# Reading the places of eight fetched batches into SP's registers a superblock ahead of the fetches

## The chip, the cores and the metric

The kernel runs on one core of one Trainium2 chip. The metric is the device time of that core in microseconds (us). Three runs of the kernel before gave 2747.27, 2744.07 and 2747.38 us; their median is 2747.27. All times inside the kernel come from one profiled execution and count from the start of its span.

## The reference

The input x holds 64 batches of 64 tokens with 256 features, and each batch has a type (0, 1 or 2). Two blocks are added to x, one after the other:

```python
x = x + attn(cond(x, itok))          # gated FFN chosen by type + shared one, gated; then attention
x = x + ffn(cond2(x, itok))          # two relu FFNs chosen by type + three shared ones, gated; then top-2 MoE
# in cond:
expert_out = einsum('bsf,bfd->bsd', gelu(h @ wi0[type]) * (h @ wi1[type]), wo[type])
weights = softmax(relu(concat([expert_out[:, 0], share_out[:, 0]]) @ g0) @ g1)
return expert_out * w0 + share_out * w1
```

All of it is in float32. What matters here is that the weights of `cond` and `cond2` depend on the batch's type, and that the result for a batch mixes a typed part and shared parts under a gate that is computed from the batch's first token.

## The kernel before

The kernel sorts the batches by type at the start, so that eight batches, a superblock of 512 tokens, share the weights of one type as far as possible. Eight superblocks (s = 0 to 7) pass through stages: the shared FFN of the first block (names with c), the typed FFN of the first block (names with e, `typed1`), the shared FFNs of the second block (names with d, `shared2`), its typed FFN (names with t, `typed2`), then the router and the MoE. Large products are made with seven half-size products instead of eight (`strassen`; tiles p1 to p7, and sa and sb for the accumulators). Small pieces of other work, above all the gates and the attention of a superblock, are put between the products: `begin_cond(s)` appends the steps of `combine1(s)` and `attention(s)` to a list, and `tick` takes one step from it.

Batches that don't fit their superblock's type are computed apart and laid beside the others in DRAM. So the typed results of a superblock go out to DRAM (`keep_typed`, into spillt) and come back one batch at a time (`fetch_typed`), each from a place that is known only at run time: the integer tile src_i holds it. In the same way the shared results of block one lie in DRAM (spill) in the order of the input and are fetched by `fetch1` in the sorted order, from the places in batch_i. Each of these fetches is a DMA of 64 KB from SP's queue, and in front of each stands a `value_load`, which takes one place from on-chip memory into a register of SP: one load (TENSOR_LOAD), one register operation and one check of the bounds (L1138, L1308). There are 64 fetches from spill and 128 from spillt, in bursts of eight: fetch1(s) once per superblock, fetch_typed(0, s) in the typed FFN of block one, and fetch_typed(1, s) in that of block two.

`fetch_typed` follows `keep_typed` in the `after` step at the end of a superblock (L1155, L1206). `fetch1(0)` is called by `begin_attention`, later ones at the end of the step `sums` of `combine1`, when its sums have read the tile part1. The first reader of what fetch1 and fetch_typed bring is the gate's first step, `hidden`: its matmuls write the tile pha in block one (tiles tw1 and part1) and phb in block two (tw and the third shared part).

SP's queue works in order. Besides these fetches it sends the weights: `send1` and `send2` (calls in `first` and `second` of each item) send the next half weights of 896 KB with their Strassen sums into a ring of five or four slots, and a load waits until TensorE has read what the slot held before. `sum_half` (L903) prepares such weights: it loads two pieces of raw weights, has POOL add four sums (`sum_weights`, L188 to L191) and writes the result to DRAM from POOL's queue (L915). Where a read and its DMA stand in SP's order is fixed by `behind_last`, which puts them behind the last DMA that `sync_dma` recorded. For the other engines a scheduler lays down the order when the program is built, from its own estimates of durations; an engine then takes its instructions in that order. POOL's queue carries, among the rest, a part of the attention: `values` (L1360) multiplies V by two masks (L1370, L1374) and copies halves across partitions by DMA (L1373), and the matmuls that write the tile ov wait for all of these. L1532 are scattered writes of x to the output.

Of the kernel before, what the change touches and what calls it, by code (L numbers as in the profile page):

```python
# [17 lines left out]
NB, S, D, F = 64, 64, 256, 1024  # L18
DC, FC = D // P, F // P
NTYPE = 3  # L20
GB = 4
NSB = NB // (2 * GB)
NG = 2 * GB
NFIX = NTYPE - 1
# [62 lines left out]
def adaln_attn_ffn(ctx: ExitStack, tc: tile.TileContext, a: dict, out: bass.AP):  # L87
    nc = tc.nc
# [9 lines left out]
    def area(kb, *shape):  # L98

        at, n = int(kb * 256), 1  # L100
        for m in shape:
            n *= m
        dims = "abcd"[: len(shape)]
        return arena[:, at : at + n].rearrange(
            f"p ({' '.join(dims)}) -> p {' '.join(dims)}", **dict(zip(dims, shape))
        )
# [21 lines left out]
    def behind_last():  # L128

        return tc.issue_after(paced["last"].ins) if paced else nullcontext()  # L130
# [166 lines left out]
    def of_half(o, g):  # L297

        return lambda op, k, i: o[op][:, k, (2 * g + i) * P : (2 * g + i + 1) * P]
# [121 lines left out]
    K = SimpleNamespace(bias={}, rows_i={})  # L421
# [11 lines left out]
    for j in range(2):  # L433
        t = area(AT_S + 14 * j, DC, F)
# [407 lines left out]
    def prepare_x(s):  # L842
        if s == 1:
            turn_x(1)
        cut_x(s)
# [9 lines left out]
    def keep1(s):  # L855
        part = area(AT_KEEP1 + 4 * (s % 2), DC, NG, S)
        v = spill[0][s * NG : (s + 1) * NG].rearrange("b p (c t) -> c p b t", c=DC)
        for c in range(DC):
            sync_dma(v[c], part[:, c])
# [10 lines left out]
    for s in range(NSB):  # L870
        its = layer(
            f"c{s}", 2, lambda g: [of_half(o, g) for o in up1],
            lambda g: lambda op, k: down1[op][:, 2 * g + k, :], lambda s=s: xblocks[s],
            AT_HOPS1, area(AT_KEEP1 + 4 * (s % 2), DC, SB), lambda s=s: keep1(s),
            (lambda s=s: prepare_x(s + 1)) if s + 1 < NSB else lambda: cut_e(0), ticks="odd",
        )
# [60 lines left out]
    def send_half(st, k, j, q, w, at):  # L937

        if (st, k) not in xes:
            with behind_last():  # L940
                r = nc.sync.value_load(K.utype_i[0:1, NSB + k : NSB + k + 1], min_val=0, max_val=NTYPE - 1)
                at_k = nc.sync.value_load(K.fix_i[0:1, k : k + 1], min_val=0, max_val=(NB - 1) * S)
            xe = area((AT_XE if st else AT_XEF) + 2 * (k % 2), DC, BT)
            n = P if k else BT
            sync_dma(xe[:, :, 0:n], X[:, :, bass.ds(at_k, n)])
            xes[st, k] = (xe, r)
        r = xes[st, k][1]
        rows = slice(q * F // 2, (q + 1) * F // 2)
        if w[0] == "i":
            t = area(at, DC, F // 2)  # L950
            src = a["L0_cond2_expert_wi"] if st else a[f"L0_cond_Wi{w[1]}"]
            src = src[bass.ds(r + j if st else r, 1), :, rows].rearrange("e (c p) f -> p (e c) f", p=P)
        else:
            t = area(at, FC // 2, D)
            src = a["L0_cond2_expert_wo"] if st else a["L0_cond_Wo"]
            src = src[bass.ds(r + j if st else r, 1), rows, :].rearrange("e (c p) d -> p (e c) d", p=P)
        sync_dma(t, src)
        ring[st, k, j, q, w] = t
# [31 lines left out]
    def send1():  # L990
        if sent1[0] == len(queue1):
            return
        kind, n, *w = queue1[sent1[0]]
        at = AT_RING1 + 7 * (sent1[0] % NRING1)
        sent1[0] += 1
        if kind == "f":
            send_half(0, n, 0, *w, at)
        elif kind == "s":
            send_share0(w[0], n, at)
        else:  # L1000
            s, g = divmod(n, 2)
            if s not in types1:
                with behind_last():
                    types1[s] = nc.sync.value_load(K.utype_i[0:1, s : s + 1], min_val=0, max_val=NTYPE - 1)
            sync_dma(
                area(at, 7 * 256), sums1[w[0]][g][bass.ds(types1[s], 1)].rearrange("e p n -> p (e n)")
            )
            ring1[n, w[0]] = half_blocks(w[0][0], at)
# [120 lines left out]
    def keep_typed(st, at, n):  # L1129
        v = spillt[st][at : at + n].rearrange("b p (c t) -> c p b t", c=DC)  # L1130
        for c in range(DC):
            sync_dma(v[c], (tp if st else tp1)[:, c, 0 : n * S].rearrange("p (b t) -> p b t", t=S))

    def fetch_typed(st, s):
        for b in range(NG):
            n = s * NG + b
            with behind_last():
                r = nc.sync.value_load(K.src_i[0:1, n : n + 1], min_val=0, max_val=NB + NFIX * GB - 1)  # L1138
                sync_dma(
                    (tw if st else tw1)[:, :, b * S : (b + 1) * S],  # L1140
                    spillt[st][bass.ds(r, 1)].rearrange("e p (c t) -> p (e c) t", c=DC),
                )

    def cut_e(s):
        xblocks["e", s], _ = column_blocks(X, s * SB, area(AT_XSUME, 4, HB))
# [3 lines left out]
    def typed1(s, ahead):  # L1149


        def ups(g):
            return [lambda op, k, i, w=w: ring1[2 * s + g, w][op][:, k, i * P : (i + 1) * P] for w in ("i0", "i1")]

        def after():  # L1155
            keep_typed(0, s * NG, NG)
            while s and s - 1 not in summed:
                tick()
            fetch_typed(0, s)

        its = layer(
            f"e{s}", 2, ups, lambda g: lambda op, k: ring1[2 * s + g, "o"][op][:, k, :],
            lambda: xblocks["e", s], AT_HOPSE, tp1, after, ahead, AT_STE, None, AT_G1E, "fine",
        )
        for it in its:
            def first(f=it.first):
                r = f()
                send1()
                send1()
                return r  # L1170

            def second(r, f=it.second):
                f(r)
                send1()

            it.first, it.second = first, second
        return its
# [8 lines left out]
    def send2():  # L1186

        if sent2[0] == len(queue2):
            return
        n, w = queue2[sent2[0]]  # L1190
        at = AT_RING2 + 7 * (sent2[0] % NRING2)
        sent2[0] += 1
        s, j, g = n // 4, n // 2 % 2, n % 2
        if s not in utypes:
            with behind_last():
                utypes[s] = nc.sync.value_load(K.utype_i[0:1, s : s + 1], min_val=0, max_val=NTYPE - 1)
        sync_dma(
            area(at, 7 * 256), sums[w][g][bass.ds(utypes[s] + j, 1)].rearrange("e p n -> p (e n)")
        )
        ring2[n, w] = half_blocks(w, at)  # L1200

    def typed2(s, ahead):
        def ups(g):
            return [lambda op, k, i: ring2[4 * s + g, "i"][op][:, k, i * P : (i + 1) * P]]

        def after():  # L1206
            while between:
                tick()
            keep_typed(1, s * NG, NG)
            fetch_typed(1, s)  # L1210

        its = layer(
            f"t{s}", 4, ups, lambda g: lambda op, k: ring2[4 * s + g, "o"][op][:, k, :],
            lambda: xblocks["d", s], AT_HOPS2[2], tp, after, ahead, AT_ST2,
            lambda g: K.wab[g // 2][:, s : s + 1],
        )
        for it in its:
            def first(f=it.first):
                r = f()
                send2()  # L1220
                return r

            def second(r, f=it.second):
                f(r)
                send2()

            it.first, it.second = first, second
        return its
# [3 lines left out]
    for j in range(4):  # L1232
        r = slice(32 * j, 32 * j + 32)
# [69 lines left out]

    def fetch1(s):
        for b in range(NG):
            n = s * NG + b
            with behind_last():
                r = nc.sync.value_load(K.batch_i[0:1, n : n + 1], min_val=0, max_val=NB - 1)  # L1308
                sync_dma(
                    part1[:, :, b * S : (b + 1) * S],  # L1310
                    spill[0][bass.ds(r, 1)].rearrange("e p (c t) -> p (e c) t", c=DC),
                )
# [311 lines left out]
    def begin_attention():  # L1624
        nc.sync.dma_start(out=g0, in_=a["L0_cond_g0"].rearrange("(c p) d -> p c d", p=P))
        nc.sync.dma_start(out=g1, in_=a["L0_cond_g1"].rearrange("(c p) j -> p c j", p=P))
        fetch1(0)

    nc.gpsimd.memset(X[:, :, NB * S : NCOL], 0.0)
# [9 lines left out]
    with tc.issue_after(K.iota.ins):  # L1639
        r = sum_columns(nc.gpsimd, up1[0], slice(0, F // 4))  # L1640
# [20 lines left out]
    for s in range(NSB):  # L1661
        its = typed1(s, (lambda s=s: cut_e(s + 1)) if s + 1 < NSB else lambda: cut_x1(0, 0))
        if s == 0:
            its = typed(0) + its
# [22 lines left out]
    for s in range(NSB):  # L1687
        its = shared2(s, 1)
# [15 lines left out]
    for s in range(NSB):  # L1704
        its = shared2(s, 2) + typed2(s, None if s == NSB - 1 else lambda s=s: cut_x1(s + 1, 2))
# [84 lines left out]
    for n, _ in enumerate(router(0)):  # L1790
        if n >= 17 and behind:
            f, _ = behind.pop(0)
# [300 lines left out]
```

## Time and profile before

| what | us |
|---|---|
| median of three runs | 2747.27 |
| the profiled execution, by the same clock | 2744.14 |
| its span in the profile | 2742.5 |
| TensorE busy (PE) | 2709.1 |
| VectorE busy (DVE) | 1626.9 |
| GpSimd busy (POOL) | 1065.2 |
| ScalarE busy (ACT) | 837.1 |
| mean granted TensorE clock | 0.999 |

A line of a view gives the source line, the engine and the operation, the tiles as written<-read, and the count. "PEld" is TensorE's weight load, "SPq" is an instruction in SP's queue, most often one that issues a DMA. In the timeline the first two columns are the start and the duration of a run of equal instructions, and the bracket at the end of a line is the idle time of the engine before it and what ended that time. Nearly all tiles are parts of one large on-chip buffer and appear as "arena". All matrix products are recorded under L119, the one line that issues them, so the tile's name tells them apart.

The five stretches that matter: the first block's shared FFN lasts until about 314 us, its typed FFN with the attention until about 840, then come the shared FFNs of block two (the first beside the last of the attention), the typed FFN of block two until about 1940, and the router and the MoE.

### The profile page before, as it was taken

The page shows a single profiled execution, that of the slowest core. Times are in us where ns is not written, and L with a number is a line of the kernel's source. Part 1 is how long each engine was busy: PE and PEld are TensorE (multiplying, and loading weights), DVE is VectorE, ACT ScalarE, POOL GpSimd, SP SyncE. Part 2 cuts the span into 40 slices and gives each one's busy share as a digit, 9 for nine tenths or more (in the row PEclk, how much of TensorE's full clock was granted, in tenths as well). Part 3 has the DMA queues.
Part 4 walks back from the last instruction along what each step waited for, and adds up shares of the span by engine and source line. Part 5 has one row for each costly group of instructions (what it writes and reads, how often), then busy time and mean ns, then how long its engine had stood idle before and what let it go on. Part 6 is the DMA issues. An engine that isn't in the chain of part 4 may idle for free.

```text
span 2742.5 us, 38338 instructions
## 1 busy us (share of the span) xinstructions
PE 2709.1 (99%) x13765; PEld 2232.6 (81%) x13765; DVE 1626.9 (59%) x2931; ACT 837.1 (31%) x1535; POOL 1065.2 (39%) x1121
## 2 busy tenths in 40 slices
PE   8999999999999999999999999999999999999998
PEld 7888887677767778888888888888888888877777
DVE  7887467888887774535546766667443333332443
ACT  2221124544444332212222222222222222322333
POOL 4555123343335667634323332325323322324332
PEclk9999999999999999999999999999999999999999
DMA  4554545343342123652443434444200000013330
GB/s 118 159 173 141 191 149 185 97 128 128 104 147 88 63 101 135 207 183 81 154 136 126 150 132 146 147 139 135 70 17 6 9 5 6 5 52 79 96 92 2
DMA packets 236365, 293.47 MB, mean 107 GB/s; under 512 B 141624, under 2 KB 199824, under 8 KB 236048
## 3 DMA queue, kind: packets, MB, share of 16 engines
q1 hardware_dynamic: 214608, 231.44, 26.9%
q0 software_dynamic: 21344, 58.54, 6.3%
q8 instruction: 109, 1.79, 0.3%
q10 hardware_dynamic: 224, 1.05, 0.1%
q14 instruction: 80, 0.66, 0.1%
HBM read 208.80 MB, written 83.99 MB: 107 GB/s over the span
## 4 chain that ended last, share of the span: by engine, by line
PE 91%; DVE 4%; issue 2%; DMA 2%; ACT 0%; SPq 0%; POOL 0%; POOLq 0%; DVEq 0%; ACTq 0%
PE sad L119 6%; PE p5r L119 5%; PE p1r L119 5%; PE po L119 5%; PE sbd L119 4%; PE sat L119 4%; PE p5d L119 3%; PE p1d L119 3%; PE sbt L119 3%; PE p6r L119 2%; PE p4r L119 2%; PE p7r L119 2%; PE p5e L119 2%; PE p1e L119 2%; PE p5t L119 2%; PE sac L119 2%
## 5 line engine op out<-in xcount | busy, mean ns | idle before, releaser
L198 POOL TENSOR_TENSOR arena<-arena 128x512 f32<-128x512 f32 (+1 forms) x175 | 236.3, 1350 | 667.2 <-DVE arena L195 659.3
L199 POOL TENSOR_TENSOR arena<-arena 128x512 f32<-128x512 f32 (+1 forms) x175 | 213.5, 1220 | 18.0 <-DVE arena L196 17.0
L119 PE MATMUL sad<-arena 128*128 128x256 f32 x768 | 176.7, 380 | 0.0
L119 PE MATMUL po<-arena 128*128 128x256 f32 (+1 forms) x704 | 169.8, 399 | 0.1
L119 PEld LDWEIGHTS sad<-arena 128*128 128x128 f32 x768 | 144.0, 190 | 19.6 <-issue 0.8
L119 PEld LDWEIGHTS po<-arena 128*128 128x128 f32 x704 | 132.9, 190 | 28.4 <-issue 11.0
L119 PE MATMUL p5r<-arena 128*128 128x256 f32 x640 | 149.7, 381 | 0.5 <-DVE arena L256 0.5
L119 PE MATMUL p1r<-arena 128*128 128x256 f32 x640 | 150.0, 382 | 0.0
L195 POOL TENSOR_TENSOR arena<-arena 128x256 f32<-128x256 f32 (+1 forms) x55 | 45.1, 821 | 260.8 <-ACT arena L1740 80.7
L1902 POOL DMA_INDIRECT xs<-arena,slot_i x64 | 62.6, 978 | 199.9 <-ACT arena L1898 108.7
L119 PEld LDWEIGHTS p1r<-arena 128*128 128x128 f32 x640 | 120.0, 190 | 21.2 <-issue 5.9
L119 PEld LDWEIGHTS p5r<-arena 128*128 128x128 f32 x640 | 120.8, 190 | 17.6 <-DVE arena L256 1.4
L119 PE MATMUL sbd<-arena 128*128 128x256 f32 x576 | 134.8, 381 | 0.0
L195 DVE TENSOR_TENSOR arena<-arena 128x512 f32<-128x512 f32 (+2 forms) x127 | 96.8, 762 | 63.2 <-ACT arena L332 34.2
L119 PEld LDWEIGHTS sbd<-arena 128*128 128x128 f32 x576 | 108.5, 190 | 17.5 <-POOL arena L199 2.2
L188 POOL TENSOR_TENSOR arena<-arena 128x256 f32<-128x256 f32 (+1 forms) x53 | 47.9, 905 | 184.8 <-DMA arena<-in_L_cond_share_wo 43.3
L119 PE MATMUL sat<-arena 128*128 128x256 f32 x512 | 118.6, 382 | 0.8 <-POOL arena L198 0.8
L196 DVE TENSOR_TENSOR arena<-arena 128x512 f32<-128x512 f32 (+2 forms) x127 | 108.8, 856 | 3.5
L2028 POOL DMA_INDIRECT out<-arena,rows_i x40 | 61.9, 1547 | 123.4 <-ACT arena L2027 66.9
L119 PEld LDWEIGHTS sat<-arena 128*128 128x128 f32 x512 | 96.2, 190 | 14.0 <-POOL arena L198 1.2
L332 ACT ACTIVATE arena<-arena 128x512 f32<-128x512 f32 x144 | 90.3, 628 | 45.6 <-DVE arena L267 21.6
L119 PE MATMUL p5d<-arena 128*128 128x256 f32 x384 | 99.7, 382 | 2.4 <-DVE arena L256 2.4
(452 smaller groups left out, 6243.5 us busy)
## 6 DMA issues: line engine op xcount, KB each, us to landing
arena<-sums_i SPq DMA_DIRECT2D x32, 896.0 KB
arena<-sums_2i SPq DMA_DIRECT2D x32, 896.0 KB
arena<-sums_2o SPq DMA_DIRECT2D x32, 896.0 KB
arena<-in_L_ffn_eW SPq DMA_DIRECT2D x16, 1024.0 KB
arena<-sums_o SPq DMA_DIRECT2D x16, 896.0 KB
spill<-arena SPq DMA_DIRECT2D x24, 512.0 KB
arena<-spill POOLq DMA_DIRECT2D x24, 512.0 KB, 6.1
sums_i<-arena POOLq DMA_DIRECT2D x12, 896.0 KB, 3.9
```

The costliest lines, as they stand in the source:

```text
L119: nc.tensor.matmul(o, lhsT=lhsT, rhs=rhs, start=start, stop=stop, skip_group_check=shared_bank)
L188: eng.tensor_add(s1, a21, a22)
L195: eng.tensor_sub(t1, b12, b11)
L196: r = eng.tensor_sub(t2, b22, t1)
L198: eng2.tensor_sub(t3, b22, b12)
L199: return r.ins, eng2.tensor_sub(t4, b21, t2).ins
L332: nc.scalar.activation(c_out(ij), src, AF.Relu)
L1902: nc.gpsimd.indirect_dma_start(out=to.rearrange("e n w -> (e n) w"), out_offset=bass.IndirectOffsetOnAxis(ap=slot_i[:, n, i : i + 1], axis=0),
L2028: nc.gpsimd.indirect_dma_start(out=out_rows, out_offset=bass.IndirectOffsetOnAxis(ap=row_i[:, u : u + 1], axis=0), in_=eo, in_offset=None, ...
```

## The change

The reads leave the fetch functions. A new function `read_ahead` reads places and keeps the registers in a dictionary; the fetches take them from there. For the typed fetches of superblock s, the reads follow the two `send1` calls of each item's `first` (two and two, so eight over the two items), or the `send2` of each of the four items' `first` in block two (two each). For the fetches of fetch1(s + 1), four reads follow the `send1` in each item's `second` of superblock s. The eight reads for fetch1(0) are made at once in `begin_attention`, directly ahead of the fetches. All reads are still made by SP with the same three instructions, and their number stays 192.

```diff
+    places = {}
+
+    def read_ahead(kind, s, bs):
+        t, top = (K.batch_i, NB) if kind == "part" else (K.src_i, NB + NFIX * GB)
+        for b in bs if s < NSB else ():
+            n = s * NG + b
+            with behind_last():
+                places[kind, n] = nc.sync.value_load(t[0:1, n : n + 1], min_val=0, max_val=top - 1)
+
     def fetch_typed(st, s):
         for b in range(NG):
-            n = s * NG + b
+            r = places.pop((st, s * NG + b))
             with behind_last():
-                r = nc.sync.value_load(K.src_i[0:1, n : n + 1], min_val=0, max_val=NB + NFIX * GB - 1)
                 sync_dma(
...
-            def first(f=it.first):
+            n = its.index(it)
+
+            def first(f=it.first, n=n):
                 r = f()
                 send1()
+                read_ahead(0, s, range(4 * n, 4 * n + 2))
                 send1()
+                read_ahead(0, s, range(4 * n + 2, 4 * n + 4))
                 return r
 
-            def second(r, f=it.second):
+            def second(r, f=it.second, n=n):
                 f(r)
                 send1()
+                read_ahead("part", s + 1, range(4 * n, 4 * n + 4))
...
-        for it in its:
-            def first(f=it.first):
+        for n, it in enumerate(its):
+            def first(f=it.first, n=n):
                 r = f()
                 send2()
+                read_ahead(1, s, range(2 * n, 2 * n + 2))
                 return r
...
     def fetch1(s):
         for b in range(NG):
-            n = s * NG + b
+            r = places.pop(("part", s * NG + b))
             with behind_last():
-                r = nc.sync.value_load(K.batch_i[0:1, n : n + 1], min_val=0, max_val=NB - 1)
                 sync_dma(
...
+        read_ahead("part", 0, range(NG))
         fetch1(0)
```

In the built program the number of instructions of each kind on SP and POOL stays as it was (one wait more on SP), and SP's DMAs keep their order. The other engines' orders differ in two places: one matmul of the tile sae stands behind the first pha instead of ahead of it, and on POOL, in the first stretch of the shared FFN, the sums L188 to L191 of one weight half and its store L915 stand ahead of, instead of behind, a group of L1370, L1374 and L1373 of the last attention superblock.

## The prediction

> **What bounds the kernel now.** First the page's row of busy times: is one engine full?
>
> ```profile
> PE 2709.1 (99%) x13765; PEld 2232.6 (81%) x13765; DVE 1626.9 (59%) x2931; ACT 837.1 (31%) x1535; POOL 1065.2 (39%) x1121
> ```
>
> TensorE is busy for 2709.1 of the 2742.5 us span, so 33.4 us is all that any change can win by removing idle time of TensorE, and a part of that lies ahead of the first matmul and behind the last. Next the waits of TensorE alone, longest first (total us, times, longest):
>
> ```profile
> PE px L831 <- POOL arena L480: 3.9, 1, 3.9
> PE p5d L119 <- DVE arena L256: 2.4, 3, 1.3
> PE pha L119 <- DMA arena<-spillt: 2.3, 1, 2.3
> ```
>
> Only the third line has to do with the transfers that the change touches: one single wait, of 2.3 us, of the gate's matmuls (pha) for the eight fetches out of spillt. The other fifteen rounds of such fetches (seven more for expert layer 1, eight for layer 2, where the gate's tile is phb) stop TensorE nowhere. Then the timeline around that wait, TensorE and SP's DMA issues:
>
> ```profile
> 414.87 0.67 PE L119 MATMUL pha<-arena 128*32 128x256 f32 x8 [2.33 <-DMA arena<-spillt]
> 415.47 2.83 PE L119 MATMUL sae<-arena 128*128 128x256 f32 x6
> 418.09 2.36 PE L119 MATMUL sbe<-arena 128*128 128x256 f32 x8
> 420.28 0.51 PE L119 MATMUL pfa<-fold,arena 128*128 128x8 f32 x4
> ```
>
> ```profile
> 402.38 10.30 SPq L126 DMA_DIRECT2D arena<-spillt  x8
> 413.51 0.99 SPq L126 DMA_DIRECT2D arena<-sums_i  x2
> ```
>
> SP needs 10.30 us to send eight fetches of 64 KB; the last leaves at about 412.1 and pha starts 2.75 us later. And behind the wait the matmuls are slow: 14 of them (6 sae, 8 sbe) take from 415.47 to 420.28, 4.81 us, where the run of 8 sae just before it (410.66) took 1.89 us, some 0.216 each from start to start. The granted clock says why (the last three columns are clock, DMA share, GB/s):
>
> ```profile
> 416.00:418.00 2.00, 2.00 (x6) 1.64 (x5) 0.00 (x0) 0.00 (x0) 1.09 (x1) 0.50 1.03 423
> ```
>
> **The reads that are moved.** A place is read by three SP instructions (durations min/median/max in ns):
>
> ```profile
> L1138 SPq TENSOR_LOAD <-src_i x128: 262/273/1072, 399.5 to 1956.7; - x128
> L1138 SPq FUSED_REGOPS  x128: 152/152/159, 400.4 to 1957.0; - x128
> L1138 SPq SEQ_ASSERT  x128: 18/18/18, 400.6 to 1957.2; - x128
> ```
>
> Together 443 ns. The pitch of the fetches is (10.30 - 0.57)/7 = 1.39 us; their own three instructions (0.037, 0.029 and the DMA's 0.568) take 0.634. What is left, 0.31 us, is hand-over between six instructions, half of it the read's: a read costs 0.60 us, a fetch without it 0.79. Nothing is removed: 192 reads (64 of batch_i, 128 of src_i) x 0.60 = 115 us of SP stay, but leave the bursts.
>
> **Step 1, the first burst.** Its start at 402.38 is set by the landing of the store into spillt, not by the first read. With a pitch of 0.79 the eighth fetch leaves at 402.38 + 7 x 0.79 = 407.9, and with the same 2.75 us pha could start at 410.7. TensorE gets to it at about 412.2 (the built program puts it one sae matmul earlier), so the wait is gone with 1.5 us to spare: 2.3 us. What is next late there? The waits written into the program behind pha are for POOL results that ended at 397.1 and 398.3 and for DVE results that ended at 411.6, all early enough.
>
> Whether the slow clock goes too is worth as much. The Trainium skill ("TensorE: Matmul & The Clock Gate", in the section "Why this matters for your kernels") asks for no idle gap over about 3 us to keep the full clock, and Part 1 has the array throttled after an idle window of about 3.4 us. By that rule a gap of 2.33 us costs no clock and the step is worth 2.3 us. The row shows 0.50 right behind this gap, and the 14 matmuls took 4.81 - 14 x 0.216 = 1.8 us too long. The row decides: step 1 is worth 2.3 + 1.8 = **4.1 us**.
>
> **Step 2, the other fifteen bursts: nothing.** Each ends 4 to 5 us earlier, ahead of gate matmuls that already found their data: pha of the second round starts at 480.8, and its last fetch left at 466.4. If this cover were gone, each would cost up to its lateness; none is near.
>
> **Step 3, where the reads go: nothing.** They stand behind weight loads (send1, send2), two or four at a time, so the load behind them leaves 1.2 or 2.4 us later; a load also waits for its ring slot, and reads in front of such a wait are free. In the timeline the shortest time from a weight load's issue to its first matmul is 6.5 us (352.4 to 358.9, and there SP stood waiting for the slot for 8 us, longer than the two reads), the next 7.7 and 8.1. The load of 7.7 (468.8 to 476.5) follows a burst that ends 4 us earlier and has six reads (3.6 us) put ahead of it, so it keeps its time. The first read of src_i gets a wait for DVE (the sort), which ended long before. Behind a waiting send1, reads only queue with what already queued there. Both ends: up to 1 us either way.
>
> **Step 4, what the reordering does to POOL: about 0.6 us lost.** Engines' instruction orders in the built program are the same except in one place of POOL, and SP's DMAs keep their order. In the first stretch of the shared FFN, POOL makes the masked values of the last attention superblock (L1370, L1374 and the copies L1373), for which TensorE's ov waits, and there the four weight sums L188 to L191 of the next weight half now stand ahead of them instead of behind:
>
> ```profile
> 861.57 1.09 POOL L1532 DMA_INDIRECT out<-arena,row_i  x1 [0.16 <-issue]
> 862.69 0.74 POOL L1370 TENSOR_TENSOR arena<-arena,vrest 128x256 f32<-128x256 f32 x1
> ...
> 873.95 0.99 POOL L188 TENSOR_TENSOR arena<-arena 128x256 f32<-128x256 f32 x1 [6.66 <-DMA arena<-in_L_cond_expert_wi]
> ```
>
> ```profile
> 848.95 10.35 SPq L126 DMA_DIRECT2D arena<-spill  x8
> 860.08 10.02 SPq L126 DMA_DIRECT2D arena<-spillt  x8
> 870.20 1.05 SPq L126 DMA_DIRECT2D arena<-in_L_cond_expert_wi  x2
> ```
>
> ```profile
> 874.23 0.66 PE L119 MATMUL ov<-arena 128*32 128x64 f32 x32
> ...
> 878.78 1.13 PE L119 MATMUL p5d<-arena 128*128 128x256 f32 x4 [0.65 <-DVE arena L256]
> ```
>
> L188 waits for a load that SP sends behind sixteen fetches. Without reads these take 16 x 0.79 = 12.6 us: the load leaves at 848.95 + 12.6 = 861.6 and L188 starts 3.75 us behind it, as before: 865.3. From there to ov, by durations of these rows: L188 1.07, L1532 1.25, L189 to L191 2.2, L1370 0.7, the store L915 0.6, L1532 1.1, first copy 0.55, L1374 0.7, second copy's landing 2.0 (the median of its six here): 10.2 us, so 875.5. TensorE stands before ov at 874.23: 1.3 us of new wait. The wait of 0.65 at 878.78 is for DVE, whose work there does not depend on ov, so it is absorbed: net 0.6. Bounds: 0, if loads come 1.3 us sooner; 2.5 idle with a slow clock behind it, some 3.7 net, if they come 1.2 us later. I take 0.6, since the gap of 1.29 us at 896.2 had clock 1.00 behind it.
>
> **Sum.** -4.1 + 0.6 = -3.5 us. The profiled execution took 2744.14 (span 2742.5 and 1.6 around it), so 2740.6; it is 3.1 below the median of the runs, 2747.27. Carried to the median: **2743.8**.
>
> **Rivals.**
> Rival 1, the stall is dearer in most executions. Two of three runs took 2747.3, 3.2 more than the profile. If that is this stall with more slow clock behind it (the clock is granted by stretches of 3.4 us, so one more costs 1.7), the change takes it away too: 2747.27 - 3.5 - 3.2 = 2740.6. For it: nothing else in the middle of the profile shows a slow clock. Against: the start shows matmuls of 0.43 us up to 12.8 us, which can vary as well.
> Rival 2, the gain is eaten. By the skill's rule the clock is not part of it (2.3), and step 4 costs 2.5 idle with its clock: between -2.3 + 0.6 and -4.1 + 3.7, so 2745.6 to 2746.9, no change that can be told.
> Rival 3, slower: the fetches do not speed up, because a 64 KB transfer and not SP's read sets the pitch; the skill ("DMA: Bandwidth & Descriptors", the section "Issuing engines are not separate DMA queues") calls issue time usually small beside the transfer. Then L188 keeps its start at 873.95, with the whole chain behind it: ov at 884.15, 9.9 us of idle TensorE plus 1.7 of slow clock, less 0.65; step 1 gives nothing, so 2747.27 + 11 = 2758; if only the late burst is stuck, 2754. It decides from a load that leaves SP later than some 869. Against it: the DMA share in a burst is 0.20, and a fetch lands 2.75 us after issue, so three or four would be in flight.
>
> **How the numbers follow.** My case 0.46, rival 1 0.30, rival 2 0.15, rival 3 0.09. Faster or slower counts from 0.2% on (5.5 us), about what a measurement of this kernel can tell from no change. Rival 1 and a fringe of my case (a dearer stall in part, 0.06) are faster; rival 3 is slower; the rest is no change. The likeliest case's own range is 2741.9 to 2746. The range of 8 in 10, 2739.5 to 2748, takes in rivals 1 and 2.
>
> **What would show it.** Right: no wait of pha for spillt, clock 1.00 from 412 to 420, bursts of 6 us, L188 near 865 less the 4 us won. Wrong: bursts still of 10 us (rival 3); a wait of ov for POOL over 2 us with clock 0.50 behind it (rival 2); a profile of after as far below 2740.6 as the run differences (rival 1).

## The result, and the profile after

The kernel became slower by 0.17%: over 20 runs each the median went from 2746.97 to 2750.33 us, and the ratio on record is 1.0017 with a 95% interval of 1.0011 to 1.0023. (The quotient of the two medians is 1.0012. The ratios in this document are the ones on record, with their intervals in brackets; the quotients of the medians lie up to 0.0006 nearer to 1.) The forecast was 2743.8 us, with 2748 as its upper end. The profiled execution of the kernel after took 2751.57 us (span 2749.9, mean clock 0.997).

TensorE is as full as before, by the page's row of busy times; its busy time grew by 2.2 us with the same number of matmuls, so some of them took longer:

```profile
PE 2711.3 (99%) x13765; PEld 2236.9 (81%) x13765; DVE 1625.2 (59%) x2931; ACT 836.9 (30%) x1535; POOL 1069.2 (39%) x1121
```

The first part of the forecast is there. In TensorE's timeline of the kernel after, pha follows the matmul ahead of it with no bracket, and the eight sae behind it take 2.00 us:

```profile
415.04 0.67 PE L119 MATMUL pha<-arena 128*32 128x256 f32 x8
415.63 2.00 PE L119 MATMUL sae<-arena 128*128 128x256 f32 x8
```

SP's timeline shows why: the bursts of eight fetches shrank from 10.3 us to about 6, and so the weight load behind two of them left at 860.60 instead of 870.20:

```profile
405.38 6.26 SPq L126 DMA_DIRECT2D arena<-spillt  x8
...
848.22 5.86 SPq L126 DMA_DIRECT2D arena<-spill  x8
854.26 6.24 SPq L126 DMA_DIRECT2D arena<-spillt  x8
860.60 1.05 SPq L126 DMA_DIRECT2D arena<-in_L_cond_expert_wi  x2
```

But in TensorE's waits the 2.3 us of pha have given way to a longer one:

```profile
PE p5d L119 <- ACT arena L1381: 5.0, 1, 5.0
```

The kernel after has 14 lines more at this place, so L1381 is L1367 of before, ScalarE's copy of pv into vn; L1384, L1387 and L1388 are L1370, L1373 and L1374; L1546 is L1532. Three timelines, of POOL, of ScalarE and of TensorE, tell the story together (start, duration, and in brackets the idle time before and what ended it):

```profile
864.38 0.73 POOL L188 TENSOR_TENSOR arena<-arena 128x256 f32<-128x256 f32 x1 [3.71 <-DMA arena<-in_L_cond_expert_wi]
...
869.28 0.72 POOL L1384 TENSOR_TENSOR arena<-arena,vrest 128x256 f32<-128x256 f32 x1
...
874.77 0.72 POOL L1388 TENSOR_TENSOR arena<-arena,vmask 64x256 f32<-64x256 f32 x1 [0.67 <-DMA out<-arena,row_i]
```

```profile
875.52 0.37 ACT L1381 COPY arena<-pv 128x256 f32<-128x256 f32 x1 [6.86 <-POOL arena L1388]
```

```profile
875.94 2.08 PE L119 MATMUL p5d<-arena 128*128 128x256 f32 x4 [4.97 <-ACT arena L1381]
```

In the kernel before, ScalarE made that copy, and TensorE began p5d, without such waits:

```profile
869.73 0.37 ACT L1367 COPY arena<-pv 128x256 f32<-128x256 f32 x1 [0.34 <-PE pv L119]
```

```profile
871.54 1.03 PE L119 MATMUL p5d<-arena 128*128 128x256 f32 x4
```

In the kernel after, POOL finishes the masked values of the first pv at 875.49 (874.77 + 0.72), since the four sums stand ahead of them. They read vn, and vn has one place (`vn = area(AT_VN, D)`). So ScalarE cannot copy the second pv before 875.52, although that pv was ready near 869. Until it is copied, pv keeps its bank of PSUM, the on-chip memory that holds the program's matmul results; pv and p5d come from one pool of four banks. By the program's waits p5d takes this bank next, so it stands still for 4.97 us. Behind the stall come slow matmuls. The windows of the kernel after (clock, DMA share, GB/s last):

```profile
416.00:418.00 2.00, 2.00 (x11) 1.77 (x10) 1.68 (x3) 0.15 (x1) 0.90 (x1) 1.00 0.92 305
872.00:880.00 8.00, 4.06 (x14) 3.57 (x15) 2.75 (x4) 1.20 (x3) 5.93 (x9) 0.57 0.35 112
903.00:907.00 4.00, 4.00 (x17) 2.22 (x17) 2.88 (x5) 1.15 (x3) 3.85 (x7) 0.58 0.32 99
```

The first row, 0.50 before, is 1.00 now. The other two are new: four matmuls of p5d took 2.08 us instead of 1.03, and a second slow stretch lies at 903, behind a wait of p5d for VectorE that grew from 1.29 us (first line, before) to 1.87 (second line, after):

```profile
896.21 1.13 PE L119 MATMUL p5d<-arena 128*128 128x256 f32 x4 [1.29 <-DVE arena L256]
902.77 1.30 PE L119 MATMUL p5d<-arena 128*128 128x256 f32 x4 [1.87 <-DVE arena L256]
```

### The profile page after: what moved, and what is told of

The parts are those of the page before. It is cut to its first block, busy times and chain, and to the rows that moved or that the text cites. A ratio compares the mean times of both kernels' runs of the same rounds, so it can differ in the third digit from the quotient of the medians.

```text
span 2749.9 us, 38338 instructions
## 1 busy us (share of the span) xinstructions
PE 2711.3 (99%) x13765; PEld 2236.9 (81%) x13765; DVE 1625.2 (59%) x2931; ACT 836.9 (30%) x1535; POOL 1069.2 (39%) x1121
## 4 chain that ended last, share of the span: by engine, by line
PE 92%; DVE 5%; issue 1%; DMA 1%; POOL 1%; ACT 0%; POOLq 0%; SPq 0%; DVEq 0%; ACTq 0%
PE sad L119 6%; PE po L119 5%; PE p5r L119 5%; PE p1r L119 5%; PE sbd L119 4%; PE sat L119 4%; PE p5d L119 3%; PE sbt L119 3%; PE p1d L119 3%; PE p6r L119 2%; PE p4r L119 2%; PE p7r L119 2%; PE p5e L119 2%; PE p1e L119 2%; PE p5t L119 2%; PE sac L119 2%
## 5 line engine op out<-in xcount | busy, mean ns | idle before, releaser
L198 POOL TENSOR_TENSOR arena<-arena 128x512 f32<-128x512 f32 (+1 forms) x175 | 237.1, 1355 | 671.4 <-DVE arena L195 663.5
L195 POOL TENSOR_TENSOR arena<-arena 128x256 f32<-128x256 f32 (+1 forms) x55 | 45.1, 820 | 271.1 <-ACT arena L1755 82.1
L195 DVE TENSOR_TENSOR arena<-arena 128x512 f32<-128x512 f32 (+2 forms) x127 | 96.3, 758 | 64.5 <-ACT arena L332 35.5
L188 POOL TENSOR_TENSOR arena<-arena 128x256 f32<-128x256 f32 (+1 forms) x53 | 49.3, 931 | 163.7 <-DMA arena<-in_L_cond_share_wo 40.1
```

What stands on the lines that cost most here:

```text
L188: eng.tensor_add(s1, a21, a22)
L195: eng.tensor_sub(t1, b12, b11)
L198: eng2.tensor_sub(t3, b22, b12)
```

## The experiments

Each ran beside the kernel before on the same chip; ratios are to that. The theory: all of the loss comes from the one reordering on POOL, by way of vn. Its rivals: the moved reads hold up SP's weight loads; or chance events (the profile of after has a 2.08 us wait of p5c for VectorE at 186 us, behind a VectorE operation at 182 that took 2.78 us instead of 0.62, ahead of every changed instruction).

**POOL's order back, reads ahead as in the kernel after.** The sums of that one weight half (`off`) are put into the program behind the masked values' last operation r. POOL's order is then that of the kernel before, but for one scattered write that changes places with L188:

```diff
...
-        sum_weights(nc.gpsimd, weight_blocks(t, at + 4))
-        nc.gpsimd.dma_start(out=to, in_=area(at, 7 * 256))
+        def sums():
+            sum_weights(nc.gpsimd, weight_blocks(t, at + 4))
+            nc.gpsimd.dma_start(out=to, in_=area(at, 7 * 256))
+
+        if off:
+            put_off.append(sums)
+        else:
+            sums()
...
+            while s == NSB - 2 and put_off:
+                with tc.issue_after(r.ins):
+                    put_off.pop()()
             return vb
...
```

> The kernel after, with all its reads ahead, but POOL's order put back: the four weight sums (L188 to L191) and their store stand behind the masked values of superblock 6 again. Theory (the whole loss is that one reordering of POOL: it keeps the single buffer vn, with it ScalarE's copy of pv, a PSUM bank and p5d, and the clock behind it): p5d near 871 waits under 0.3 us, clock 1.00 from 866 to 880, and about 4.1 us less than the kernel before (ratio 0.9985). Rival 1 (the reads behind weight loads make SP late): the time stays 3 to 5 us above before (ratio 1.001 to 1.002), and the p5d wait's disappearance is made up by waits for weight loads. Rival 2 (chance events such as the 2 us wait of p5c at 183 us in the profile of after make the difference): within 1 us of after whatever happens at 871.

Measured: 2742.89 us against 2745.16, ratio 0.9987 (0.9977 to 0.9996). TensorE's timeline has no bracket at this place, and the clock of 870 to 876 is 1.00:

```profile
867.53 1.03 PE L119 MATMUL p5d<-arena 128*128 128x256 f32 x4
...
870.23 0.66 PE L119 MATMUL ov<-arena 128*32 128x64 f32 x32
```

The same 192 reads at the same places, and the slowdown is a gain. The reads behind weight loads are not the cause, and neither is chance: the interval lies clear of that of the kernel after. The gain is less than the 4.1 us that were expected (2.3 by the medians), though the interval still takes 4.1 in; where the rest went is taken up with the sum below.

**Two places for vn, POOL's order as after.**

```diff
-            vn = area(AT_VN, D)
+            vn = area(171 if s == NSB - 2 and i % 2 else AT_VN, D)
```

> The kernel after, POOL order unchanged, but in superblock 6 every second vn lies in a place of its own, so that ScalarE's copy of the second pv need not wait for POOL. Theory: the copy starts near 869, the 5.0 us wait of p5d is gone with the slow clock behind it (3.4 us), and nothing binds in its place, as ov's values are ready at 875.5 and TensorE gets to ov near 875.6: 4 us less than before (ratio 0.9985). If the chain of my prediction over the masked values to ov binds as well, ov waits 1.3 us: 2.8 us less than before. Rival (the loss has nothing to do with vn): time as after, ratio 1.0017.

Measured: 2744.92 us, ratio 0.9995 (0.9985 to 1.0005); against the kernel after's 1.0017 that is 6 us won back by one buffer (some 4 by the medians). The wait of p5d for ScalarE is gone. What binds in its place is the chain of the prediction, from L188 over the masked values to ov:

```profile
873.39 0.32 PE L119 MATMUL ov<-arena 128*32 128x64 f32 x8 [1.60 <-DMA arena<-arena]
873.92 0.54 PE L119 MATMUL ov<-arena 128*32 128x64 f32 x24 [0.21 <-POOL arena L1388]
```

Together 1.81 us, where 1.3 was predicted for that wait. This profile also has a slow stretch at 896.9, again behind a wait of p5d for VectorE (1.88 us), which the profile of the first experiment does not have.

**Only the first burst's eight reads ahead, on the kernel before.**

```diff
...
+            r = places.pop(n, None) if st == 0 else None
             with behind_last():
-                r = nc.sync.value_load(K.src_i[0:1, n : n + 1], min_val=0, max_val=NB + NFIX * GB - 1)
+                if r is None:
+                    r = nc.sync.value_load(K.src_i[0:1, n : n + 1], min_val=0, max_val=NB + NFIX * GB - 1)
...
                 r = f()
                 send1()
+                if s == 0:
+                    read_ahead(range(4 * n, 4 * n + 2))
                 send1()
+                if s == 0:
+                    read_ahead(range(4 * n + 2, 4 * n + 4))
```

> The kernel before, with only the eight reads of the first typed burst moved ahead (superblock 0, block one); the other 184 reads stay in front of their fetches, and POOL's order is that of before. Theory: pha's wait of 2.3 us and the slow clock behind it (1.8 us) go, nothing else moves: 4.1 us less than before (ratio 0.9985). By the rule that only gaps over 3 us cost clock: 2.3 us less. Rival 2 (the time differs by chance events, and this stall is filled by others later): no change, 1.0000.

Measured: 2742.64 us, ratio 0.9985 (0.9974 to 0.9996), which does not tell 4.1 us from 2.3. The profile does: pha waits no more, no half clock follows, and the matmuls behind it lie 4.1 us earlier than those ahead of it, both against the kernel before:

```profile
411.42 0.67 PE L119 MATMUL pha<-arena 128*32 128x256 f32 x8
412.02 1.99 PE L119 MATMUL sae<-arena 128*128 128x256 f32 x8
```

Step 1 is as predicted, with its clock. Its profile also holds a wait of 3.75 us (plga, for VectorE, at 759), which is taken up below.

**Both mends together.** The edits of the first two experiments.

> Both mends together: POOL's order of before and two places for vn in superblock 6, on the kernel after. Theory: as with POOL's order alone, 4.1 us less than before (ratio 0.9985), because each mend alone takes the same wait away. If each takes only a part away, it is the fastest of all, by 1 us or more below the other two.

Measured: 2742.40 us, ratio 0.9987 (0.9977 to 0.9997), the same as POOL's order alone: with POOL's order back, the second place for vn adds nothing. The two mends take away one and the same wait.

**POOL's new order alone, no read moved.** `put_off` holds the store L915 of that weight half; the copies and the products with vmask that follow are moved with the first product.

```diff
...
-            nc.gpsimd.tensor_mul(vx, vn, K.vrest.rearrange("p a b d -> p (a b d)"))
+            late = s == NSB - 2 and i == 0 and put_off
+            with tc.issue_after(put_off[0].ins) if late else nullcontext():
+                nc.gpsimd.tensor_mul(vx, vn, K.vrest.rearrange("p a b d -> p (a b d)"))
...
```

> The kernel before, with every read still in front of its fetch, and only POOL's order changed: in superblock 6 the first masked values (L1370, L1374, L1373) stand behind the four weight sums and their store, as in the kernel after. Theory (the order is what costs, and reads ahead only soften it): the sums still wait for the late load and start near 874, the masked values are done near 882, so ScalarE's copy of the second pv and with it p5d wait until about 882: 11 us of idle TensorE, plus 2 to 3.4 us of slow clock, less 0.65: 12 to 14 us more than the kernel before (ratio 1.0045 to 1.005). Rival (the order alone is harmless, it needs the moved reads): within 2 us of before.

Measured: 2756.43 us against 2745.41, ratio 1.0043 (1.0029 to 1.0057), about 11 us slower, just under the 12 to 14 that were expected. ScalarE stands idle for 11.89 us ahead of its copy, and in this build the tile that waits for the bank is ppT, which comes from the same pool, not p5d:

```profile
879.60 0.37 ACT L1371 COPY arena<-pv 128x256 f32<-128x256 f32 x1 [11.89 <-POOL arena L1380]
```

```profile
869.86 1.03 PE L119 MATMUL p5d<-arena 128*128 128x256 f32 x4
880.03 1.97 PE L1425 MATMUL ppT<-ident,arena 128*128 128x128 f32 x8 [9.14 <-ACT arena L1371]
```

So the order is harmful by itself, and the moved reads, which send the load some 10 us earlier, soften it.

**Two places for vn on the kernel before, a control.** The edit of the second experiment.

> A control: the kernel before with two places for vn in superblock 6 and nothing else. Theory: vn's single place keeps nobody waiting in POOL's old order, so 1.0000, within 1 us. If vn's place were worth time by itself, the gain of two places on the kernel after could not be put down to the reordering.

Measured: 2745.75 us, ratio 1.0001 (0.9991 to 1.0011). In POOL's old order vn keeps nobody waiting.

**POOL's order back, and the next half's sums later too.** In the first experiment the p5d wait for VectorE near 892 is still 1.88 us, against 1.29 in the kernel before. VectorE's timeline of the kernel before and then of that experiment, the same two operations of the softmax:

```profile
890.38 1.28 DVE L1402 TENSOR_TENSOR arena<-arena,mx 128x512 f32<-128x512 f32 x2
...
893.61 1.94 DVE L1407 TENSOR_TENSOR arena<-arena,sm 128x512 f32<-128x512 f32 x2
```

```profile
885.83 2.08 DVE L1427 TENSOR_TENSOR arena<-arena,mx 128x512 f32<-128x512 f32 x2
...
889.85 2.23 DVE L1432 TENSOR_TENSOR arena<-arena,sm 128x512 f32<-128x512 f32 x2
```

They became longer by 0.80 and 0.29 us. POOL's sums L188 to L191 of the next weight half run from 886.3 to 889.9 there, beside them; in the kernel before they ran from 892.3 to 896.1. The edit makes these sums wait for the last masked values of superblock 6 (`with tc.issue_after(values_done[-1])`).

> The kernel after with POOL's order put back, and also the four sums of the next weight half (L188 near 886) put behind the last masked values of superblock 6, some 10 us later. Theory (a VectorE operation with two on-chip inputs is held up while POOL works, so sums that run beside the softmax products L1427 and L1432 delay VectorE's L256 and with it p5d near 892): L1427 near 886 takes 1.28 us for two instead of 2.08, p5d near 892 waits 1.3 us or less instead of 1.88 and has full clock behind it, and the kernel takes 1 to 2 us less than with POOL's order alone, 5 to 6 us less than before (ratio 0.998). Rival (those operations are long for another reason): their durations and the wait stay, same time as with POOL's order alone.

Measured: 2741.83 us, ratio 0.9985 (0.9976 to 0.9994). In the profile the two operations take 1.53 and 1.91 us, p5d waits 1.50, with clock 1.00 behind it. The direction is the theory's. The size for these operations is less; other POOL work (L195 to L198 and L1393) slid into the place, which is likely why. From 880 to 908 the matmuls of this profile lose 0.4 us against the kernel before, where with POOL's order alone they lose 2.0. The run time cannot be told from that of the first experiment.

**The kernel after again, unchanged.**

> The kernel after once more, unchanged. Theory: the wait of p5d for ScalarE's copy near 871 (5 us) is there again, in the same size and with the slow clock behind it, and the time is 3 to 5 us above before; the wait of p5c near 183 us, which belongs to no changed instruction, need not be there. If the 871 wait is missing while the time stays the same, my theory falls.

Measured: 2749.93 us, ratio 1.0019 (1.0010 to 1.0028). The wait is there again, with clock 0.50 from 871 to 877; the wait of p5c is not:

```profile
873.48 2.07 PE L119 MATMUL p5d<-arena 128*128 128x256 f32 x4 [5.10 <-ACT arena L1381]
```

So the first belongs to the change. The second comes and goes: a wait of p5c of 1.92 us stands at 185.5 in the profile of both mends, and one of 2.65 us at 228.5 in that of the control, the kernel before with two places for vn.

## Why the prediction was wrong

The second profile of the kernel after is free of p5c's wait, so the sum is checked in it: by how much the same matmuls lie later than in the kernel before (rounded). The column beside it has the same for the first experiment, POOL's order back.

| stretch of before, us | change of the delay | the same, POOL's order back | what the prediction had |
|---|---|---|---|
| 0 to 400, ahead of the first typed burst | +0.4 | -0.4 | 0 |
| 400 to 420, pha | -4.1 | -4.1 | -4.1 (step 1) |
| 420 to 769, other bursts and reads | +0.3 | +0.6 | 0 (steps 2 and 3) |
| 769 to 871, p5d | +5.3 | -0.1 | 0 |
| 871 to 880, slow clock there, less the old 0.65 wait | +1.1 | -0.5 | -0.65 |
| ov's wait for the masked values | hidden behind p5d | none | +1.3 |
| 880 to 908, waits for VectorE and, in the kernel after, a slow clock | +3.1 | +2.0 | 0 |
| 908 to the end | -1.2 | 0.0 | 0 |
| sum | +5.0 | -2.6 | -3.5 |

From 400 on, the first profile of the kernel after has the same rows within 0.2 us. The row 0 to 400 is chance: it goes from -1.9 to +4.2 us over the nine profiles of the experiments and of the kernel after, and nearly all of that comes ahead of 300 us, where no read had moved. So the sum of a single profile says less than its rows.

Step 1 was right in mechanism and size, the half clock included: the row of before decided against the rule of a 3 us gap, and the experiment with the first burst alone shows the same 4.1 us in its profile. Steps 2 and 3 were right: the bursts take 5.8 to 7.0 us, and no weight load appears in TensorE's waits of the kernel after.

**Step 4 failed.** It was booked as +0.6, bounds 0 to 3.7, and measured +8.3 from 769 on. With POOL's order put back, +1.3 of this is left, so the order accounts for 7.0. Three things were in it.

First, the chain was followed to the wrong reader. The prediction worked out that ov would find its values at 875.5, which is 26.6 us behind the start of the first burst at 848.95. In the kernel after that burst starts at 848.22, and POOL finished them 27.3 us later. That the clock then reads 875.49 is luck, since the kernel after runs 0.7 us ahead there; but the chain, as far as it went, was only 0.7 us too short. The experiment with two places for vn shows it at work: ov waits 1.81 us, not 1.3. But the late operations also read vn, and the next writer of vn, ScalarE's copy of the second pv, waits for them; behind it hangs a PSUM bank and TensorE, at p5d, which stands three groups of matmuls ahead of ov. ScalarE's copy had 0.34 us of idle time before it in the kernel before, and it stood in the timeline. The question "who reads the result" was asked, the question "who may overwrite the input" was not.

Second, "the wait of 0.65 is absorbed": it came back at the next wait of p5d for VectorE. In the first experiment, without any stall at 871, the 0.54 us gained at 879 are followed by a loss of 1.08 up to 896, while the next half's sums, which moved with the load, run beside VectorE's softmax operations, and of another 0.92 at 904, where plga waits for VectorE. So 2.0 us between 880 and 908 do not hang on vn. The experiment with the later sums, where 0.4 is left of them, speaks for POOL's sums as the cause, in one profile.

Third, a slow clock was allowed for as a bound but not booked. It came twice, behind the 5 us stall and behind the 1.87 us wait.

The prediction, and the text ahead of it, called this attention superblock the last; it is superblock 6, the last but one. No number hangs on that.

Rival 1, a stall that is dearer in most executions, was not borne out: without step 4 it asks for 7.3 us (4.1 + 3.2) from the first burst alone, a ratio of 0.9973, just outside the interval of that experiment, and in all three profiles that have the stall (the kernel before, the control and POOL's new order alone) a single stretch of 3.4 us of half clock lies behind it. Rival 2, the gain eaten by step 4, had the right place but not the right price (2745.6 to 2746.9): it also took ov as the waiter. Rival 3, the only slower one, rested on fetches that do not speed up; they did (eight in 6.26 us instead of 10.30), so SP's issuing and not the 64 KB transfer had set the pitch. The version that beats both kernels is the kernel after with POOL's order put back, with or without the later sums: 0.9985 to 0.9987 of before.

## What to carry to other kernels

When a change moves work in a queue, list for each late instruction not only who reads what it writes, but who is waiting to overwrite what it reads: a single buffer turns a late reader into a stall of the producer, and of whatever the producer still holds. A wait that "goes" should be followed to the next wait for the same engine before it is booked as a gain. And a scheduler's reordering far from the edit is part of the edit; holding it back is a cheap experiment.

## What the runs showed of the hardware

**The half clock comes in windows on a fixed grid.** In each run the half-clock windows last 3.413 us or a multiple (apart from the one that runs past the end of the span), and their starts in one run lie whole multiples of 3.413 apart (in the kernel after 186.80, 872.88 and 903.60: 201 and 9 steps). The Trainium skill ("TensorE: Matmul & The Clock Gate", "What's actually happening") calls this window free-running, which agrees. What does not agree is the gap of over about 3 us that the prediction took from the same page: gaps of 1.87 to 2.65 us had a half clock behind them in nine cases (of all gaps behind the first 25 us), while gaps of 1.81 us and less had none. And three gaps of 1.87 or 1.88 us (POOL's order back, both mends, POOL's new order alone) had none either: carried back on the grid from the last slow window of each run, a boundary falls inside each of these three, so that no window held more than 1.45 us of them. That reading, idle time counted window by window, fits each gap that began a half clock here and each that did not, but no run was made to test it. It does not say how long the half clock lasts: in the profile of the first burst alone a second half-clock window follows one with only 1.08 us of idle time.

**VectorE operations that become long beside POOL.** What held up p5c at 186 us, in VectorE's and then POOL's timeline of the kernel after:

```profile
181.92 2.78 DVE L739 SCALAR_TENSOR_TENSOR arena<-arena 128x64 f32<-128x64 f32 x1
```

```profile
182.12 1.28 POOL L198 TENSOR_TENSOR arena<-arena 128x512 f32<-128x512 f32 x1
183.34 1.27 POOL L199 TENSOR_TENSOR arena<-arena 128x512 f32<-128x512 f32 x1
```

L739 took 0.62 us in the kernel before, 0.28 with POOL's order back, and 2.62 with both mends, where p5c waits as well; here it ends at 184.70, just behind two POOL operations that end at 184.61. By the Trainium skill ("SBUF — State Buffer", "Who interferes with whom") a VectorE operation with two on-chip inputs and a GpSimd operation that reads on-chip memory exclude each other, which agrees. The 3.75 us wait in the profile of the first burst alone has the same sign: two L1417 took 5.97 us instead of the 1.92 of before while POOL worked with hardly a break. VectorE operations that read one input from PSUM (L242, L251, 0.69 us on average) show none of this. That such collisions make the scatter of the runs (2739 to 2753 us for the kernel before) is likely, but not shown.
